# Four graph-attention layers on one core: engines that issue in text order, a third buffer for the rows, and 33-column sums in the third layer

## The chip, the cores and the metric

The kernel runs on one NeuronCore of a Trainium2 chip. The metric is the time of one execution on the device, in microseconds (us). A core has a matrix engine (TensorE, in the profile PE, with its weight loads as PEld), a vector engine (VectorE, DVE), an activation engine (ScalarE, ACT), a general engine (GpSimd, POOL) and a queue that only starts transfers (SyncE, SP). Each takes its own list of instructions in the order in which the compiler has put them, and they wait for each other by semaphores.

## The reference

The input x has 8 batches of 2048 rows with 128 features; adj is a 2048x2048 symmetric 0/1 matrix, shared by all batches. Four layers follow one another, each of the form x = x + layer(relu(layernorm(x))).

- Layers 0 and 1 are graph attention: Wh = h W, a score leaky_relu(f1[i] + f2[j]) for each pair of rows, a softmax over the j that are neighbours of i, and the weighted sum of Wh. Layer 0 ends with elu.
- Layer 2 has no weights: 4 heads of 32 features, score = leaky_relu(h_i . h_j), softmax over neighbours, weighted sum of h itself.
- Layer 3 is graph attention again, with the rows scaled by node weights before it, a layernorm after the projection, that normed value added to the sum, and elu.

```
scores = einsum('bihk,bjhk->bhij', x, x); scores = leaky_relu(scores, 0.2)
probs = softmax(where(adj == 0, -inf, scores)); out = einsum('bhij,bjhk->bihk', probs, x)
```

## The kernel before

**Units.** A unit is one layer of one batch. Even and odd batches form two streams, and the units alternate between them, so that while one unit computes its attention, the next one, of the other batch, is prepared. Numbered in the order of execution: unit 0 is batch 0 layer 0, 1 is batch 0 layer 1, 2 is batch 1 layer 0, 3 is batch 0 layer 2, 4 is batch 1 layer 1, 5 is batch 0 layer 3, 6 is batch 1 layer 2, 7 is batch 2 layer 0, 8 is batch 1 layer 3, 9 is batch 2 layer 1, 10 is batch 3 layer 0, 11 is batch 2 layer 2, and so on with a period of eight; unit 31 is batch 7 layer 3. Units 0 and 1, and 30 and 31, are of the same batch, so that 1 and 31 are prepared with nothing beside them.

**Steps.** A unit has steps, each with a front and a back. For layers 0, 1 and 3 (`Gat`, 16 steps) front(s) makes a tile z of masked attention weights with two VectorE instructions of 128x1024 (L455), and back(s) is 16 matmuls of z against the 129-column y (L468; the last column gives the softmax's denominator). For layer 2 (`Heads`, 4 groups of 512 rows, 16 steps each) front(s) is eight score matmuls (L539, a value split into two parts, hi_lo and lo_hi), two exponentials on ACT (L542) and one mask product on VectorE (L544); back(s) is the sums (L557): for each head a 32-column block of hv and a 32-column block of ones, each in its own 32-column tile of the array. z has three buffers. The text writes front(s+2) ahead of back(s).

**PSUM.** The eight banks are shared out by hand: score pairs start at banks 6, 4 and 2 in turn (`score_banks`), Heads sums in banks 0 and 1, Gat sums of the first eight row blocks in 5, 6, 7 and of the second eight in 2, 1, 0. Preparation uses the single pair 3,4 while a Gat unit runs, and the score pairs in turn while a Heads unit runs.

**Preparation.** `begin` of the next unit is a list of pieces, called one by one after the steps: with P pieces, ceil(P(s+1)/(steps-4)) of them have been called after step s. It has 20 pieces for layers 0 and 1, 17 for layer 2 and 39 for layer 3: the statistics of x, four row blocks at a time (`stats`, L193 and L194), `end` (variance on VectorE, a power on POOL at L201, a product at L203), `rows` (ACT, L245), for layer 3 `scaled` (L252), `turned` (eight transposes L263, copied by ACT), and then `project` (L287), `spread` (L338), and for layer 3 a second round of statistics, `normed` and `weighted`. For layer 2 `kept` copies the rows to hv and `stacked` issues sixteen copies on SP's queue from the two parts of the transposed rows to hi_lo and lo_hi (L277, L278). In a Gat unit that is followed by a Heads unit, front(0) of the latter stands in the text ahead of the last back, and front(1) behind it.

**Ends.** When a half of a Gat unit is done, `out_first` (L396) divides and evacuates it, and `out_elu` or, for layer 3, `out_norm` and then the output's transfer follow some steps later by `later` and `pass_time`. When a group of a Heads unit is done, ACT copies the two banks of sums (L563), and `out` takes the reciprocal of 128x512 denominators (L567), multiplies (L568), transposes (L571) and adds to x (L573).

**Order.** Nothing of this text order binds the engines: a planner, working from estimated costs, priorities and free buffers, chooses the order in which each engine issues, and puts in the semaphores. It follows the text in the middle of a Heads unit and departs from it elsewhere: VectorE's statistics are moved ahead of mask products, PE's transposes and projections behind sums, and the four transposes of L571 some 35 PE instructions back. The eight batches' rows x have two buffers, so that the load of a third batch waits for the output of the first.

Of the kernel before, what the change touches and what calls it, by code (L numbers as in the profile page):

```python
# [8 lines left out]
F32 = mybir.dt.float32  # L9
# [5 lines left out]
OP = mybir.AluOpType  # L15
# [4 lines left out]
HD = 32  # L20
SLOPE = 0.2
# [13 lines left out]
def adj_preln_d4(ctx: ExitStack, tc: tile.TileContext, x, adj, w0, a0, w1, a1, w3, a3,  # L35
# [80 lines left out]
    beta2_sb = const.tile([P, C], F32, name="beta2_sb")  # L116
    nc.vector.tensor_scalar(beta2_sb, beta_sb, 2.0, None, op0=OP.mult)
# [20 lines left out]
    def run(ctx, general):  # L138
# [25 lines left out]
        def load_x(b):  # L164
            X[b] = big.tile([P, NB, C], F32, tag="x", name="x")
            nc.sync.dma_start(out=X[b], in_=x[b].rearrange("(n p) c -> p n c", p=P))
# [21 lines left out]
        hv = held.tile([P, NB, C], F32, name="hv")  # L188
# [17 lines left out]
        class Unit:  # L206
# [5 lines left out]
            def begin(self, banks):  # L212
# [42 lines left out]
                def kept(half):  # L255
                    nc.vector.tensor_copy(hv[:, half * HB:(half + 1) * HB, :], self.hw[half])
# [164 lines left out]
            def out_norm(self, half, xs, a, later):  # L421
                nc.vector.tensor_add(a, a, self.wh[:, half * HB:(half + 1) * HB, :])
                nc.vector.tensor_mul(a, a, gamma_sb[:, None, :].to_broadcast([P, HB, C]))
                nc.vector.tensor_add(a, a, beta2_sb[:, None, :].to_broadcast([P, HB, C]))
# [100 lines left out]
        class Heads(Unit):  # L525
# [22 lines left out]
            def back(self, s, later):  # L548


                g, jb = divmod(s, NB)
                z = self.z.pop(s)
                for bank in range(2):
                    for h in range(HEADS):
                        cols = slice(h * HD, (h + 1) * HD)
                        lhsT = ones[:, cols] if bank else hv[:, jb, cols]
                        nc.tensor.matmul(ps[cols, bank, :], lhsT=lhsT, rhs=z[:, h, :],  # L557
                                         start=(jb == 0), stop=(jb == NB - 1),
                                         tile_position=(0, h * HD))
                if jb == NB - 1:  # L560
                    o_t = big.tile([P, 2, 512], F32, tag="o_t", name="o_t")
                    for bank in range(2):
                        nc.scalar.copy(o_t[:, bank, :], ps[:, bank, :])  # L563
                    later(2.6, lambda: self.out(g, o_t))

            def out(self, g, o_t):
                nc.vector.reciprocal(o_t[:, 1, :], o_t[:, 1, :])  # L567
                nc.vector.tensor_mul(o_t[:, 0, :], o_t[:, 0, :], o_t[:, 1, :])  # L568
                pv = ps[:, score_banks(), :].rearrange("p (k e) -> p k e", k=4)
                for k in range(4):  # L570
                    nc.tensor.transpose(pv[:, k, :], o_t[:, 0, k * P:(k + 1) * P], ident)  # L571
                xs = X[self.b][:, g * 4:g * 4 + 4, :]
# [94 lines left out]
```

## Time and profile before

The median of two runs is 3630.32 us (3630.07 to 3630.56). The profiled execution took 3630.07; its span from the first to the last instruction is 3628.3, and the mean clock granted to TensorE is 0.954.

| | us |
|---|---|
| PE / PEld busy | 3326.6 / 2225.2 |
| DVE / ACT / POOL busy | 2760.0 / 1675.7 / 134.7 |
| L468, Gat sums, PE | 1424.1 |
| L557, Heads sums, PE: hv, ones | 580.3, 572.4 |
| L544 mask, L542 exponentials | 1167.3, 1083.3 |
| L567 reciprocal, 32 of 3346 ns | 107.1 |
| the chain that ended last: PE / DVE / ACT | 65% / 17% / 9% |

The units in the steady part, from the first matmul of one unit's back to that of the next: 3 (Heads) from 347.7 to 559.5, 211.8 long; 4 to 631.1, 71.6; 5 to 706.5, 75.4; 6 (Heads) to 923.7, 217.2; 7 to 995.1, 71.4; 8 to 1060.0, 64.9; 9 to 1132.2, 72.2; 10 to 1215.8, 83.6. Unit 28 takes 72.5 and unit 1 65.4; unit 30 computes from 3314.0 to 3516.2.

In a group's line the mean of one instruction is in ns, and "idle before" is the time its engine stood ahead of it, with the releaser that ended it. In a timeline, the first two numbers are start and length in us, "x8" is so many instructions taken together, and the bracket is the idle time ahead. A float32 matmul appears as two passes, so that L557 has 4096 entries for 2048 matmuls. PE busy is not PE at its peak, as overlapping matmuls count once.

### The profile page before, as it was taken

To read this page: it belongs to the slowest core of one execution; us is meant where nothing else is said; L and a number is where in the kernel's file an instruction comes from. 1 tells how busy PE (TensorE), PEld (TensorE's weight loads), DVE (VectorE), ACT (ScalarE), POOL (GpSimd) and SP (SyncE) were. 2 spreads that over 40 slices of the span, in tenths; PEclk is the share of its full clock that TensorE was granted. 3 is DMA by queue.
4 is the path that set the end of the run, shared out by engine and by line. 5 is a ranking of instruction groups with operands and counts; after the bars stand their busy time and mean duration, and the time that the engine had idled before them with its cause. 6 is when DMAs were issued, how large, how long until landed. Compare 5 with 4: busy or idle time off the path is not lost.

```text
span 3628.3 us, 61084 instructions
## 1 busy us (share of the span) xinstructions
PE 3326.6 (92%) x26637; PEld 2225.2 (61%) x26637; DVE 2760.0 (76%) x3490; ACT 1675.7 (46%) x2521; POOL 134.7 (4%) x46
## 2 busy tenths in 40 slices
PE   4798999999999899989999899999999989999987
PEld 3796338733899334943499733783379943495337
DVE  3666778777887677867797677877788768787876
ACT  4214663376422564256442366426642256524652
POOL 0000000000000000000000000000000000010000
PEclk7888999999999899989999899999999989999998
DMA  6002000300000200030000200020000020002000
GB/s 212 1 1 47 1 1 1 71 1 1 1 24 5 43 1 1 1 70 1 1 1 24 47 1 1 1 71 1 1 1 7 19 47 1 1 1 59 1 1 13
DMA packets 35541, 71.46 MB, mean 20 GB/s; under 512 B 8000, under 2 KB 25024, under 8 KB 29120
## 3 DMA queue, kind: packets, MB, share of 16 engines
q1 hardware_dynamic: 29312, 67.12, 7.2%
q8 instruction: 210, 3.44, 0.4%
q10 hardware_dynamic: 5952, 0.35, 0.1%
q14 instruction: 67, 0.55, 0.0%
HBM read 25.51 MB, written 8.39 MB: 9 GB/s over the span
## 4 chain that ended last, share of the span: by engine, by line
PE 65%; DVE 17%; ACT 9%; issue 3%; POOL 3%; DMA 2%; POOLq 0%; ACTq 0%; DVEq 0%; SPq 0%
PE ps L468 28%; PE ps L557 20%; PE ps L539 12%; ACT z L542 5%; DVE z L544 5%; DVE z L455 4%; DVE o_t L567 3%; PE ps L287 2%; POOL rstdx L201 2%; PE ps L263 2%; ACT wh L321 1%; PE ps L338 1%; ACT hw L245 1%; DVE stx L193 1%; POOL rstdh L201 1%
## 5 line engine op out<-in xcount | busy, mean ns | idle before, releaser
L544 DVE TENSOR_TENSOR z<-z,edge_t 128x2048 f32<-128x2048 f32 x512 | 1167.3, 2288 | 396.2 <-ACT z L542 396.1
L468 PE MATMUL ps<-y,z 128*128 128x129 f32 x12288 | 1424.1, 277 | 4.0 <-DVE z L455 4.0
L468 PEld LDWEIGHTS ps<-y,z 128*128 128x128 f32 x12288 | 1405.5, 193 | 14.7 <-DVE z L455 5.9
L542 ACT ACTIVATE z<-ps,shift 128x1024 f32<-128x1024 f32 x1024 | 1083.3, 1113 | 492.7 <-PE ps L539 471.5
L455 DVE SCALAR_TENSOR_TENSOR z<-r,cr,edge_t 128x1024 f32<-128x1024 f32 x768 | 951.7, 1275 | 86.1 <-PE ps L468 73.6
L557 PE MATMUL ps<-z,hv 128*32 128x512 f32 x4096 | 580.3, 615 | 25.2 <-DVE z L544 23.0
L539 PE MATMUL ps<-hi_lo 64*128 64x512 f32 x2048 | 497.3, 461 | 111.9 <-ACT z L542 103.4
L557 PE MATMUL ps<-z,ones 128*32 128x512 f32 x4096 | 572.4, 599 | 0.0
L539 PEld LDWEIGHTS ps<-hi_lo 64*128 64x128 f32 x2048 | 206.3, 188 | 565.9 <-ACT z L542 433.9
L245 ACT ACTIVATE hw<-x,nmrx,rstdx 128x128 f32<-128x128 f32 x512 | 203.7, 482 | 547.3 <-DVE nmrx L203 547.3
L539 PE MATMUL ps<-lo_hi,hi_lo 64*128 64x512 f32 x2048 | 432.1, 402 | 0.0
L557 PEld LDWEIGHTS ps<-z,ones 128*32 128x32 f32 x4096 | 136.8, 111 | 311.7 <-issue 310.9
L539 PEld LDWEIGHTS ps<-lo_hi,hi_lo 64*128 64x128 f32 x2048 | 214.5, 191 | 22.1
L557 PEld LDWEIGHTS ps<-z,hv 128*32 128x32 f32 x4096 | 85.0, 108 | 226.8 <-issue 155.3
L201 POOL TENSOR_TENSOR rstdx<-varx,neg_half 128x16 f32<-128x16 f32 x32 | 104.2, 3258 | 3206.5 <-DVE varx L199 3206.5
L263 PE MATMUL ps<-ident,hw 128*128 128x128 f32 x512 | 96.1, 305 | 54.4 <-ACT hw L245 26.7
L193 DVE BATCH_NORM_STATS2 stx<-x 128x6 f32<-128x128 f32 x512 | 127.6, 268 | 12.6 <-DMA x<-in_x_dram 11.6
L412 ACT ACTIVATE oe<-ps,rs 128x128 f32<-128x128 f32 x128 | 52.4, 409 | 177.5 <-DVE rs L405 177.5
L287 PEld LDWEIGHTS ps<-rhs,h_t 128*128 128x128 f32 x768 | 102.3, 204 | 49.1 <-issue 14.3
L287 PE MATMUL ps<-rhs,h_t 128*128 128x130 f32 x768 | 120.5, 300 | 10.2 <-DVE y L299 6.7
L415 ACT ACTIVATE oa<-ps,rs 128x128 f32<-128x128 f32 x128 | 35.3, 380 | 180.1 <-DVE rs L405 180.1
L263 PEld LDWEIGHTS ps<-ident,hw 128*128 128x128 f32 x512 | 66.3, 150 | 77.7 <-ACT hw L245 30.6
(89 smaller groups left out, 1267.7 us busy)
## 6 DMA issues: line engine op xcount, KB each, us to landing
raw<-in_adj_dram SPq DMA_DIRECT2D x16, 1024.0 KB, 7.3
hi_lo<-h_hi SPq DMA_DIRECT2D x32, 256.0 KB, 5.1
hi_lo<-h_lo SPq DMA_DIRECT2D x32, 256.0 KB, 5.1
lo_hi<-h_lo SPq DMA_DIRECT2D x32, 256.0 KB, 5.1
lo_hi<-h_hi SPq DMA_DIRECT2D x32, 256.0 KB, 5.2
out_dram<-x SPq DMA_DIRECT2D x16, 512.0 KB, 3.3
w_sb<-in_L_gnn_W_dram ACTq DMA_DIRECT2D x3, 64.0 KB, 2.3
x<-in_x_dram SPq DMA_DIRECT2D x8, 0.5 KB, 6.4
```

The costliest lines, as they stand in the source:

```text
L193: nc.vector.bn_stats(out=st[:, n, :], in_=block(n))
L201: nc.gpsimd.tensor_tensor(out=rstd, in0=var, in1=neg_half, op=OP.pow)
L245: nc.scalar.activation(h, self.xb[:, n, :], AF.Relu, scale=self.rstd[:, n:n + 1], bias=self.nmr[:, n:n + 1])
L263: nc.tensor.transpose(pk[:, k, :], self.hw[half][:, k, :], ident)
L287: nc.tensor.matmul(pv[:, k, :C + 2], lhsT=self.h_t[:, n * P:(n + 1) * P], rhs=rhs, start=True, stop=True)
L455: nc.vector.scalar_tensor_tensor(z[:, j, :], self.r[:, sl], self.cr[:, 0, jb:jb + 1], edge_t[:, jb, sl], op0=OP.max, op1=OP.mult)
L468: nc.tensor.matmul(ps[:, SUMS[half][i // 3], k * CE:(k + 1) * CE], lhsT=z[:, j, i * P:(i + 1) * P], rhs=self.y[:, jb, :], start=(jb == 0 a ...
L539: nc.tensor.matmul(ps[:, lo + h, :], lhsT=hi_lo[rows, pair, js], rhs=rhs[rows, pair, ts], start=rhs is hi_lo, stop=rhs is lo_hi)
L542: nc.scalar.activation(z[:, pair * 2:pair * 2 + 2, :], ps[:, lo:lo + 2, :], AF.Exp, bias=shift)
L544: nc.vector.tensor_mul(z, z, edge_t[:, jb, None, ts].to_broadcast([P, HEADS, 512]))
L557: nc.tensor.matmul(ps[cols, bank, :], lhsT=lhsT, rhs=z[:, h, :], start=(jb == 0), stop=(jb == NB - 1), tile_position=(0, h * HD))
L567: nc.vector.reciprocal(o_t[:, 1, :], o_t[:, 1, :])
```

## The change

Four things change together.

- Inside the branch that runs, PE, ACT and DVE issue in the order of the text (`manual_schedule`). SP and POOL keep the planner's order.
- x has three buffers. To make room, twice beta is computed in place.
- hv gets 33 columns a head, the last one 1.0 (a memset on POOL at the start); `kept` copies into the first 32 of each.
- The sums of a head are one matmul with 33 columns, two heads to a bank, at partitions 0 and 64; four matmuls instead of eight. `out` is called for each pair of heads: four transposes, a reciprocal of the 128x8 denominators, a product into a new tile, and the sum into x; each call takes a turn of the score banks.

```diff
-            X[b] = big.tile([P, NB, C], F32, tag="x", name="x")
+            X[b] = big.tile([P, NB, C], F32, tag="x", name="x", bufs=3)
...
-        hv = held.tile([P, NB, C], F32, name="hv")
+        hv = held.tile([P, NB, HEADS, HE], F32, name="hv")
+        nc.gpsimd.memset(hv[:, :, :, HD:HE], 1.0)
...
-                for bank in range(2):
-                    for h in range(HEADS):
-                        cols = slice(h * HD, (h + 1) * HD)
-                        lhsT = ones[:, cols] if bank else hv[:, jb, cols]
-                        nc.tensor.matmul(ps[cols, bank, :], lhsT=lhsT, rhs=z[:, h, :],
-                                         start=(jb == 0), stop=(jb == NB - 1),
-                                         tile_position=(0, h * HD))
-                if jb == NB - 1:
-                    o_t = big.tile([P, 2, 512], F32, tag="o_t", name="o_t")
-                    for bank in range(2):
-                        nc.scalar.copy(o_t[:, bank, :], ps[:, bank, :])
-                    later(2.6, lambda: self.out(g, o_t))
-
-            def out(self, g, o_t):
-                nc.vector.reciprocal(o_t[:, 1, :], o_t[:, 1, :])
-                nc.vector.tensor_mul(o_t[:, 0, :], o_t[:, 0, :], o_t[:, 1, :])
-                pv = ps[:, score_banks(), :].rearrange("p (k e) -> p k e", k=4)
+                for pair in range(2):
+                    for h in range(2):
+                        nc.tensor.matmul(ps[h * 64:h * 64 + HE, pair, :],
+                                         lhsT=hv[:, jb, pair * 2 + h, :], rhs=z[:, pair * 2 + h, :],
+                                         start=(jb == 0), stop=(jb == NB - 1))
+                    if jb == NB - 1:
+                        o_t = big.tile([P, 512], F32, tag="o_t", name="o_t")
+                        nc.scalar.copy(o_t, ps[:, pair, :])
+                        later(2.6, lambda o_t=o_t, pair=pair: self.out(g, pair, o_t))
+
+            def out(self, g, pair, o_t):
+                lo = score_banks()
+                pv = ps[:, lo, :].rearrange("p (k e) -> p k e", k=4)
                 for k in range(4):
-                    nc.tensor.transpose(pv[:, k, :], o_t[:, 0, k * P:(k + 1) * P], ident)
-                xs = X[self.b][:, g * 4:g * 4 + 4, :]
-                nc.vector.tensor_add(xs, xs, pv)
+                    nc.tensor.transpose(pv[:, k, :], o_t[:, k * P:(k + 1) * P], ident)
+                pv = pv.rearrange("p k (h e) -> p k h e", h=2)
+                r = stat.tile([P, 4, 2, 1], F32, tag="r2", name="r2")
+                nc.vector.reciprocal(r, pv[:, :, :, HD:HE])
+                o = big.tile([P, 4, 2, HD], F32, tag="o", name="o", bufs=1)
+                nc.vector.tensor_mul(o, pv[:, :, :, :HD], r.to_broadcast([P, 4, 2, HD]))
+                xs = X[self.b][:, g * 4:g * 4 + 4, pair * 64:(pair + 1) * 64]
+                nc.vector.tensor_add(xs, xs, o.rearrange("p k h d -> p k (h d)"))
...
+            inner.enter_context(tc.manual_schedule(engines={
+                mybir.EngineType.PE, mybir.EngineType.Activation, mybir.EngineType.DVE}))
             run(inner, False)
```

## The prediction

> **What bounds the kernel now.** I read the page first (shares, slices), then the stretches unit by unit (units are numbered in the text above), then timelines of single steps. The page:
>
> ```profile
> PE 3326.6 (92%) x26637; PEld 2225.2 (61%) x26637; DVE 2760.0 (76%) x3490; ACT 1675.7 (46%) x2521; POOL 134.7 (4%) x46
> ...
> PE   4798999999999899989999899999999989999987
> PEld 3796338733899334943499733783379943495337
> DVE  3666778777887677867797677877788768787876
> ```
>
> PE is busy 92% on average, but the share is not one limit throughout. Units 4, 8, 9 and 30 (columns: length, then busy us of PE, PEld, DVE, ACT):
>
> ```profile
> 559.50:631.10 71.60, 66.51 (x585) 65.07 (x582) 64.43 (x142) 19.61 (x44) 7.65 (x2) 1.00 0.01 1
> ...
> 995.10:1060.00 64.90, 64.78 (x578) 64.40 (x577) 52.65 (x67) 19.86 (x59) 3.78 (x1) 1.00 0.03 9
> 1060.00:1132.20 72.20, 68.22 (x578) 67.48 (x577) 57.22 (x107) 15.15 (x40) 3.78 (x1) 0.95 0.08 23
> ...
> 3314.00:3516.20 202.20, 197.30 (x1520) 69.92 (x1520) 160.54 (x96) 132.84 (x130) 0.00 (x0) 0.99 0.00 1
> ```
>
> Unit 8 is PE and nothing else. Unit 4, a Gat unit that prepares a layer-3 unit, is VectorE: 64.43 busy and two waits of 2.79 for POOL's rstd make 70.0 of 71.6. A Heads step is PE's:
>
> ```profile
> 423.44 2.29 DVE L544 TENSOR_TENSOR z<-z,edge_t 128x2048 f32<-128x2048 f32 x1 [0.69 <-ACT z L542]
> 423.50 0.50 PE L539 MATMUL ps<-hi_lo 64*128 64x512 f32 x2
> ...
> 424.30 2.12 ACT L542 ACTIVATE z<-ps,shift 128x1024 f32<-128x1024 f32 x2 [0.88 <-PE ps L539]
> ...
> 424.63 1.06 PE L557 MATMUL ps<-z,hv 128*32 128x512 f32 x8
> 425.51 1.04 PE L557 MATMUL ps<-z,ones 128*32 128x512 f32 x8
> 426.48 0.50 PE L539 MATMUL ps<-hi_lo 64*128 64x512 f32 x2
> ```
>
> 2.98 us a step, of which the sums take 424.63 to 426.48, 1.85; the mask (2.29) and the exponentials (2.12) fit beneath. A Gat step is 3.57 (16 matmuls in two passes, "x128" in 14.3 for four steps) over 2.46 of VectorE. So 24 x 57.2 + 8 x 190.7 = 2898 of the 3628.3; the rest is preparation and stalls. The two places where PE stands:
>
> ```profile
> 1172.40 1.04 PE L263 MATMUL ps<-ident,hw 128*128 128x128 f32 x8
> ...
> 1176.51 1.22 DVE L268 TENSOR_TENSOR h_lo<-ps,h_hi 128x1024 fp32r<-128x1024 f32 x1
> ...
> 1193.94 1.28 SPq L278 DMA_DIRECT2D lo_hi<-h_hi  x1
> ...
> 1207.60 0.79 PE L539 MATMUL ps<-hi_lo 64*128 64x512 f32 x1 [12.94 <-ACT z L542]
> ```
>
> Gat to Heads (unit 10): the copies into hi_lo and lo_hi go out at about 1.25 apiece, and PE waits 12.94 for exponentials queued behind other ACT work. The end of a Heads group:
>
> ```profile
> 3363.60 3.34 DVE L567 RECIPROCAL o_t<-o_t 128x512 f32<-128x512 f32 x1
> ...
> 3369.15 1.04 PE L557 MATMUL ps<-z,hv 128*32 128x512 f32 x2 [1.01 <-DVE z L544]
> 3370.12 0.66 PE L571 MATMUL ps<-ident,o_t 128*128 128x128 f32 x4
> ```
>
> The reciprocal holds the mask. Unit 30 is 202.2 against 190.7: 11.5 for three group ends inside it, 3.8 each.
>
> **What the Trainium skill says.** "TensorEngine Tiling (Array Packing)", Available Configurations: 128x32 gives four tiles, 128x64 two, working independently. The trace agrees for four: eight passes begin 0.88 apart per set of four heads, two slots of 0.43. No row shows two of 64. "TensorE: Matmul & The Clock Gate", the table at its head: ACT and VectorE queues are strict FIFO, PE pulls only weight loads ahead; so an instruction that waits holds all behind it. The 12.94 agrees. Same page, Part 1: some 3.4 us of idling halves the clock. Agrees: after that stall hv's eight took 1.94 for 1.06.
>
> **The sums (L557).** Removed: eight matmuls in four-wide tiles, four slots of 0.43. Added: four with 33 columns, two-wide: again 8 passes / 2 = four slots. Unchanged at 1.85, if two 64-column tiles run side by side. Bound: from 0 to +1.7 a step (one after another, 8 x 0.43 = 3.44), 512 steps. I take 0.
>
> **Group ends.** Removed: L567 (3.34), L568 (0.68), L573 (0.69), four transposes. Added, for each pair: four transposes (0.53 to 0.66), a reciprocal of 128x8 (0.17, as L405), a product and a sum of 128x256 (0.4 each, from L573's 0.69 for twice the size), and a second turn of the score banks. In text order they stand right after the last sums: PE waits for the ACT copy behind the second exponential (0.55), transposes twice (1.15), and the second score pair waits 0.6 for the bank that VectorE still reads. 2.35 for 3.8: -1.45, x32 = -46.
>
> **The order.** All stretches below are the text laid out by hand with these durations: z pair 2.46; statistics of four blocks 1.5 (a dependent pair of L193 and L194 is 0.38, where the planner's interleaving shows 0.29); "end" 3.8 to 4.2 (POOL 2.90 to 3.79 and both semaphores), during which VectorE stands with everything behind it; scaled 1.1; weighted 0.69; norm_end 5.0. Pieces fall at ceil(count(s+1)/12) a step.
> Unit 4 (39 pieces): on VectorE, out 1.9, z(2) 4.4, three statistics 8.9, z(3) 11.4, statistics and end 16.7, z(4) 19.2. PE has done back(3) at 15 and waits 4.2 for z(4); then 1.2 for turned, 1.1 and three times 1.0 in project, since bank pair 3,4 is single: back(7) ends at 44.5. VectorE then does recips, products, norm_stats and norm_end up to 60.8, z(11) at 63.3: PE waits 2.6 and 5.4, two spreads 3.2, four more steps: 84.4 for 71.6. Before, 12 of the 16 statistics were done in the Heads unit's VectorE slack. Same for unit 7 (71.4). +12.9 each; ends +6 to +16.
> Unit 8 (20 pieces), on VectorE: z(2), a statistic and unit 7's out_elu 6.4; z(3) 8.9; two statistics 11.9; z(4) and a statistic 15.9; z(5) and end 22.5; z(6) 25.0. PE, with back(5) from 18.4, has done it at 22.0 and waits 3.0 for z(6) (0.5 before that). So 57.2, 8.8 of PE pieces (two turned of 1.1, four projects of 1.15, two spreads of 1.0), 3.5, and 2.6 where two pieces on bank pair 3,4 stand in one step = 72.1 for 64.9, +7.2. Unit 9 is the same with out_norm (3.7) and out_elu (2.4) of layer 3 in its first three steps: waits of 7.3 for 3.5, 75.9 for 72.2, +3.7.
> Unit 10: 41.3 to the second turned, +3.7 behind layer 1's L409s and end. Then front(0) stands in the text before back(15). The copies land 20.9 after L268 ends (1177.7 to 1198.6), L268 ends 2.3 after turned: 23.2, and PE is there after four steps, 14.3. So it waits 8.4, with back(15) behind it; back(15) ends at about 29.8 (3.57 and 2.5 of slow clock), the copies out of banks 2,1,0 and the exponential of front(1) hold back(0) for 5.1 more: 34.9 for 42.4. 79.9 for 83.6, -3.7. Unit 5: the out DMA ahead of the copies on SP's queue makes the same wait 13: 82.6 for 75.4, +7.2.
> Units 3, 6: 190.7, four ends 9.4, PE pieces 9.7, end 1.2, and 2 in unit 6 for out_norm: 211.0 and 213.0 for 211.8 and 217.2: -0.8, -4.2.
> Sum of units 3 to 10: +35.2 (2 x 12.9 + 7.2 + 3.7 - 3.7 + 7.2 - 0.8 - 4.2). Three such rounds: +105.6. Units 27 to 30: -0.8 + 11.9 + 7.2 + 0 (ends -5.8, the unhidden start of unit 31 +6). Unit 0: x's statistics now follow all sixteen edge casts, +9. Units 1, 2: +4.5, -3.7. Together +134.
>
> **The third x buffer.** SP waited 17.2 in six loads for the out DMA. Text order would put VectorE behind such a load; with three buffers the load stands at the unit's start, hidden by the unit before. Nothing taken; up to 9 (6.1 landing, 3.2) in each of three units if it is issued late.
> **Else.** The hv copy with a gap every 32 (16 x 0.7), the memset and doubling beta in place: nothing, at most 7 on VectorE in Heads slack.
>
> 3628.3 + 134 = 3762, and 1.8 around the span as before (3630.07 for 3628.3): **3764**. The profiled run is 0.25 below the median, nothing at this size.
>
> **Rivals.**
> Faster: the wait at Gat to Heads goes. If the copies have landed when PE comes to front(0), it leaves Gat at once: units of type 10 lose 17.3, of type 5 11, four each, -113, with the ends -46: 3471 if VectorE also keeps up, 3496 with half the cost of units 8 and 9 (16) and unit 0's start (9). It decides at 14.3 us from turned to the last landing; 23.2 measured speaks against. 0.09.
> Balanced: VectorE keeps its two z ahead, as its total falls by 107 + 22 + 22 (L567, L568, L573) against some 60 added; then units 4 and 7 cost +4 (7 x 9 less) and 8 and 9 half (16 less): 3685, within 3590 to 3703. Unit 4's 70.0 of 71.6 speaks against: what the order takes from the Heads units has no room there. 0.17.
> Serial tiles: the 64-column tiles take turns: +1.6 to 1.7 x 512 less some VectorE waits it hides: 4600. 0.08.
> That the order is not what the text says is excluded for steady Heads steps, where both orders are the same.
>
> **How the numbers follow.** Forecast 0.66, 3703 to 3860, with units 4 and 7 and tile switches at their ends. Range 3590 to 3860 leaves out faster and serial. A measurement tells about 2% (73 us) from no change: slower 0.66 + 0.08, same 0.17, faster 0.09.
>
> **What would show it.** L557 still 1.85 a step, statistics evenly in Gat units, PE waiting for z L455 there some 10 us a unit; L539 waiting for the copies' DMA before the last Gat step; no 3.3 us reciprocal. Wrong if unit 4 stays near 72, or a Heads step isn't 2.98.

## The result, and the profile after

The changed kernel takes 3789.27 us (median of 2 runs, 3787.88 to 3790.66) for 3630.32 before: a ratio of 1.0438, 95% interval 1.0393 to 1.0483. It is slower by 159 us. The forecast was 3764 and slower; the sum was 25 us short, with one stall not foreseen, others mis-sized and two terms that were set at nothing. The profiled execution took 3787.88, its span is 3786.1, and the mean clock granted to TensorE 0.944 (0.954 before).

The page after: engine totals, TensorE's slices, and the two groups of matmuls with the most idle time ahead of them (the last figures of a group line are that idle time, with its releasers). The same two groups before stand below.

```profile
PE 3325.6 (88%) x22669; PEld 2246.7 (59%) x22669; DVE 2743.8 (72%) x3586; ACT 1681.6 (44%) x2521; POOL 117.0 (3%) x47
...
PE   4798998799899899979988899888989989988986
...
L471 PE MATMUL ps<-y,z 128*128 128x129 f32 x12288 | 1465.4, 282 | 115.3 <-DVE z L458 114.9
...
L542 PE MATMUL ps<-hi_lo 64*128 64x512 f32 x2048 | 473.6, 452 | 127.4 <-DMA hi_lo<-h_lo 50.5
```

Before:

```profile
L468 PE MATMUL ps<-y,z 128*128 128x129 f32 x12288 | 1424.1, 277 | 4.0 <-DVE z L455 4.0
...
L539 PE MATMUL ps<-hi_lo 64*128 64x512 f32 x2048 | 497.3, 461 | 111.9 <-ACT z L542 103.4
```

PE is busy for the same time as before (3326.6), VectorE for 16 us less, ACT for 6 more: over the whole span, the 158 us are time in which PE stands. Gat's sums now wait 115 us, nearly all of it for VectorE's z, where they waited 4. The first passes of the scores wait 127 us for 112, so there it is mainly the reasons that changed: exponentials before, and now the copies with 50 as the largest of three. The second passes (lo_hi) wait 25.5 us for the copies, where they waited for nothing, and the projections (L290, L287 before) wait 43.7 for 10.2.

A wait also costs what comes after it. Gat's sums are the same matmuls as before and are busy for 1465.4 us instead of 1424.1. Cut into short stretches, the profile has a granted clock of 1.00 in steady steps (401 to 404) and of 0.5 to 0.6 behind the long waits (0.51 from 588.7 to 594.0 in unit 4). That PE's total did not rise is owed to the changed kernel's other matmuls: without the text's order it keeps PE busy for 3306.9 only, at a clock of 0.961 (the run of the sums and the buffer below).

Unit by unit, from one back's first matmul to the next (us):

| units | before | forecast | after |
|---|---|---|---|
| start of unit 0, and unit 0 | 102.0 + 96.7 | 9 more | 107.5 + 100.2 |
| 3 (Heads) | 211.8 | 211.0 | 210.9 |
| 4 (Gat, prepares layer 3) | 71.6 | 84.4 | 84.9 |
| 5 | 75.4 | 82.6 | 81.1 |
| 6 (Heads, behind layer 3) | 217.2 | 213.0 | 219.5 |
| 7 | 71.4 | 84.3 | 85.2 |
| 8 | 64.9 | 72.1 | 72.9 |
| 9 | 72.2 | 75.9 | 74.2 |
| 10 | 83.6 | 79.9 | 81.6 |
| 30 with the preparation of 31 | 240.0 | 240.2 | 249.5 |

The steady Heads step is what it was. In the timeline (start, length, instruction, idle time ahead) the masks of two steps stand 2.97 apart (2.98 before). The eight passes of the 33-column sums take 1.91 to their end and 1.84 to the start of the next scores (401.46 to 403.30), where the eight and eight of before took 1.85 to the next scores.

```profile
401.46 1.91 PE L556 MATMUL ps<-z,hv 128*33 128x512 f32 x8
...
403.30 0.50 PE L542 MATMUL ps<-hi_lo 64*128 64x512 f32 x2
...
428.48 2.29 DVE L547 TENSOR_TENSOR z<-z,edge_t 128x2048 f32<-128x2048 f32 x1 [0.67 <-ACT z L545]
...
431.45 2.29 DVE L547 TENSOR_TENSOR z<-z,edge_t 128x2048 f32<-128x2048 f32 x1 [0.68 <-ACT z L545]
```

The first end of a group in unit 3:

```profile
404.43 1.91 PE L556 MATMUL ps<-z,hv 128*33 128x512 f32 x8
406.08 1.07 ACT L561 COPY o_t<-ps 128x512 f32<-128x512 f32 x2
...
406.72 1.14 PE L568 MATMUL ps<-ident,o_t 128*128 128x128 f32 x8 [0.38 <-ACT o_t L561]
...
408.43 0.17 DVE L200 TENSOR_SCALAR varx<-mvx 128x16 f32<-128x16 f32 x1
...
408.77 2.90 POOL L202 TENSOR_TENSOR rstdx<-varx,neg_half 128x16 f32<-128x16 f32 x1 [110.92 <-DVE varx L200]
411.70 0.18 DVE L204 SCALAR_TENSOR_TENSOR nmrx<-mvx,rstdx 128x16 f32<-128x16 f32 x1 [3.10 <-POOL rstdx L202]
...
412.03 0.42 DVE L573 TENSOR_TENSOR o<-ps,r 128x256 f32<-128x256 f32 x1
...
412.51 0.50 PE L542 MATMUL ps<-hi_lo 64*128 64x512 f32 x2 [3.98 <-DVE o L573]
...
413.26 3.46 PE L556 MATMUL ps<-z,hv 128*33 128x512 f32 x8
```

The 3.34 us reciprocal is gone, and at the next two ends PE stands 0.6 at the scores where here it stands 3.98. What makes this one long is `end`: the variance, POOL's power and the product stand in the text ahead of `out`, VectorE waits for POOL, and the product L573 that frees the bank of the next scores waits behind it. The sums that follow then take 3.46 for 1.91, as the granted clock is 0.54 from 413.2 to 416.7.

The two unit types that lost most are 4 and 7. In unit 4, VectorE works off twelve blocks of statistics in a row (from 575.15), and then `end`:

```profile
579.91 2.45 DVE L458 SCALAR_TENSOR_TENSOR z<-r,cr,edge_t 128x1024 f32<-128x1024 f32 x2
581.21 3.84 PE L471 MATMUL ps<-y,z 128*128 128x129 f32 x32 [1.20 <-DVE z L458]
...
583.99 0.18 DVE L200 TENSOR_SCALAR varx<-mvx 128x16 f32<-128x16 f32 x1
584.34 2.90 POOL L202 TENSOR_TENSOR rstdx<-varx,neg_half 128x16 f32<-128x16 f32 x1 [172.67 <-DVE varx L200]
587.27 0.17 DVE L204 SCALAR_TENSOR_TENSOR nmrx<-mvx,rstdx 128x16 f32<-128x16 f32 x1 [3.10 <-POOL rstdx L202]
587.37 2.47 DVE L458 SCALAR_TENSOR_TENSOR z<-r,cr,edge_t 128x1024 f32<-128x1024 f32 x2
...
588.70 1.66 PE L471 MATMUL ps<-y,z 128*128 128x129 f32 x6 [3.64 <-DVE z L458]
...
631.34 2.87 PE L471 MATMUL ps<-y,z 128*128 128x129 f32 x12 [4.47 <-DVE z L458]
```

PE stands for 1.20 and 3.64 here, for 1.16 and 4.47 around `norm_end` (the last line), and four times for 0.9 to 1.1 at transposes and projections: 14.4 in all. The unit as a whole (length, busy us of PE, PEld, DVE, ACT, POOL, then clock, share of the DMA engines, GB/s):

```profile
569.10:654.00 84.90, 70.47 (x578) 68.84 (x577) 65.94 (x152) 19.24 (x43) 5.80 (x2) 0.94 0.00 1
```

Before, unit 4 had PE busy for 66.51 of 71.6 at a clock of 1.00. So of the 13.3 us that it lost, 9.3 are more waiting and 4.0 are matmuls that took longer behind the waits.

Unit 6 holds what the forecast did not have:

```profile
742.40 1.22 DVE L427 TENSOR_TENSOR oa<-oa,beta_sb 128x1024 f32<-128x1024 f32 x1
743.72 1.06 ACT L429 ACTIVATE oe<-oa 128x1024 f32<-128x1024 f32 x1 [6.26 <-DVE oa L427]
744.81 1.06 ACT L430 ACTIVATE oa<-oa 128x1024 f32<-128x1024 f32 x1
745.77 4.11 ACT L545 ACTIVATE z<-ps,shift 128x1024 f32<-128x1024 f32 x4
746.92 0.79 PE L542 MATMUL ps<-hi_lo 64*128 64x512 f32 x2 [6.22 <-ACT z L545]
```

`out_norm` of unit 5 issues an exponential and a relu on ACT behind three VectorE instructions, and those stand behind two masks. ACT waits for them, the score exponentials L545 wait behind ACT's two, and PE stands for 6.22 us. It is so in units 6, 14, 22 and 30.

In unit 8 the longest wait is a projection (L290) that needs the single bank pair 3,4:

```profile
1082.75 1.06 ACT L430 ACTIVATE oa<-oa 128x1024 f32<-128x1024 f32 x1
...
1084.03 0.69 DVE L302 TENSOR_TENSOR y<-ps,y 128x512 f32<-128x512 f32 x1
...
1084.77 1.51 PE L290 MATMUL ps<-rhs,h_t 128*128 128x130 f32 x8 [3.46 <-DVE y L302]
```

At the turn from Gat to Heads (unit 2), the scores of front(0) stand ahead of the last sums:

```profile
339.10 0.79 PE L542 MATMUL ps<-hi_lo 64*128 64x512 f32 x1 [2.00 <-DMA hi_lo<-h_lo]
...
344.13 0.76 PE L542 MATMUL ps<-hi_lo 64*128 64x512 f32 x1 [4.25 <-DMA hi_lo<-h_lo]
...
346.55 0.76 PE L542 MATMUL ps<-lo_hi,hi_lo 64*128 64x512 f32 x1 [1.53 <-DMA lo_hi<-h_hi]
...
347.24 5.91 PE L471 MATMUL ps<-y,z 128*128 128x129 f32 x32
```

With the 1.22 before them these waits make 9.0, and the sums that had been ready then run in 5.91 for 3.57, at a granted clock of 0.64.

### The profile page after: what moved, and what is told of

The parts are those of the page before. It is cut to its first block, busy times and chain, and to the rows that moved or that the text cites. A ratio compares the mean times of both kernels' runs of the same rounds, so it can differ in the third digit from the quotient of the medians.

```text
span 3786.1 us, 53159 instructions
## 1 busy us (share of the span) xinstructions
PE 3325.6 (88%) x22669; PEld 2246.7 (59%) x22669; DVE 2743.8 (72%) x3586; ACT 1681.6 (44%) x2521; POOL 117.0 (3%) x47
## 4 chain that ended last, share of the span: by engine, by line
PE 62%; DVE 18%; ACT 5%; issue 2%; POOL 2%; SPq 2%; DMA 1%; POOLq 0%; DVEq 0%; ACTq 0%
PE ps L556 22%; PE ps L471 22%; PE ps L542 14%; DVE z L458 8%; ACT z L545 2%; PE ps L290 2%; DVE z L547 2%; POOL rstdx L202 2%; DMA lo_hi<-h_hi 1%; DVE stx L194 1%; DVE mvx L195 1%; PE ps L341 1%; PE ps L266 1%; SPq L280 1%; SPq L281 1%
## 5 line engine op out<-in xcount | busy, mean ns | idle before, releaser
L471 PE MATMUL ps<-y,z 128*128 128x129 f32 x12288 | 1465.4, 282 | 115.3 <-DVE z L458 114.9
L471 PEld LDWEIGHTS ps<-y,z 128*128 128x128 f32 x12288 | 1445.0, 199 | 131.5 <-DVE z L458 128.0
L545 ACT ACTIVATE z<-ps,shift 128x1024 f32<-128x1024 f32 x1024 | 1087.7, 1114 | 610.5 <-PE ps L542 605.7
L556 PE MATMUL ps<-z,hv 128*33 128x512 f32 x4096 | 995.0, 608 | 8.2 <-DVE z L547 8.2
L542 PE MATMUL ps<-hi_lo 64*128 64x512 f32 x2048 | 473.6, 452 | 127.4 <-DMA hi_lo<-h_lo 50.5
L556 PEld LDWEIGHTS ps<-z,hv 128*33 128x33 f32 x4096 | 197.8, 111 | 531.7 <-issue 495.3
L246 ACT ACTIVATE hw<-x,nmrx,rstdx 128x128 f32<-128x128 f32 x512 | 206.0, 488 | 559.9 <-DVE nmrx L204 559.9
L542 PE MATMUL ps<-lo_hi,hi_lo 64*128 64x512 f32 x2048 | 419.9, 397 | 25.5 <-DMA lo_hi<-h_hi 25.5
L542 PEld LDWEIGHTS ps<-lo_hi,hi_lo 64*128 64x128 f32 x2048 | 199.4, 188 | 53.6 <-issue 24.8
L290 PE MATMUL ps<-rhs,h_t 128*128 128x130 f32 x768 | 118.1, 302 | 43.7 <-DVE y L302 21.6
L290 PEld LDWEIGHTS ps<-rhs,h_t 128*128 128x128 f32 x768 | 102.3, 207 | 75.3 <-DVE y L302 24.7
L266 PE MATMUL ps<-ident,hw 128*128 128x128 f32 x512 | 77.6, 292 | 41.4 <-ACT hw L246 24.5
L195 DVE BATCH_NORM_AGGREGATE mvx<-stx 128x2 f32<-128x6 f32 x512 | 93.2, 182 | 17.8
L302 DVE TENSOR_TENSOR y<-ps,y 128x512 f32<-128x512 f32 x64 | 44.1, 688 | 84.1 <-ACT cr L397 83.9
```

The source lines that it names most:

```text
L195: nc.vector.bn_aggr(out=mv[:, n, :], in_=st[:, n, :])
L246: nc.scalar.activation(h, self.xb[:, n, :], AF.Relu, scale=self.rstd[:, n:n + 1], bias=self.nmr[:, n:n + 1])
L266: nc.tensor.transpose(pk[:, k, :], self.hw[half][:, k, :], ident)
L290: nc.tensor.matmul(pv[:, k, :C + 2], lhsT=self.h_t[:, n * P:(n + 1) * P], rhs=rhs, start=True, stop=True)
L471: nc.tensor.matmul(ps[:, SUMS[half][i // 3], k * CE:(k + 1) * CE], lhsT=z[:, j, i * P:(i + 1) * P], rhs=self.y[:, jb, :], start=(jb == 0 a ...
L542: nc.tensor.matmul(ps[:, lo + h, :], lhsT=hi_lo[rows, pair, js], rhs=rhs[rows, pair, ts], start=rhs is hi_lo, stop=rhs is lo_hi)
```

## Experiments: which part of the change costs

The theory: the text's order is the cause, VectorE's above all; the sums are neutral in the steady step and cheaper at group ends; the third buffer is worth nothing. The rivals: the two-wide sums are the cause; or PE's and ACT's order is.

**The order with the old sums.** The kernel before, with the third buffer (and, to make room, o_t with one buffer and twice beta in place) and the text's order.

```diff
-            X[b] = big.tile([P, NB, C], F32, tag="x", name="x")
+            X[b] = big.tile([P, NB, C], F32, tag="x", name="x", bufs=3)
...
-                    o_t = big.tile([P, 2, 512], F32, tag="o_t", name="o_t")
+                    o_t = big.tile([P, 2, 512], F32, tag="o_t", name="o_t", bufs=1)
...
+            inner.enter_context(tc.manual_schedule(engines={
+                mybir.EngineType.PE, mybir.EngineType.Activation, mybir.EngineType.DVE}))
```

> The kernel before with its own sums (eight matmuls in 32-column tiles, the 128x512 reciprocal), a third buffer for x (one buffer fewer for o_t makes the room) and the text's order on PE, ACT and DVE. Theory (the order is the cause): at least as slow as the changed kernel, because the whole loss of 159 us is the order's, and the group ends, which the new sums made cheaper, stay: the reciprocal of 3.34 us then stands between the last sums and the transposes with nothing moved into its place, 32 ends of some 5 us where the changed kernel has some 2.3 to 4: 3810 to 3900 us. Rival (the two-wide sums are what costs): near 3630, within 40.

Measured: 3975.76 us, ratio 1.0941 (1.0923 to 1.096), past the upper end of what the theory gave. Heads units take 236 to 246, where the changed kernel's take 209 to 220. The first end of a group in its unit 3, in its timeline:

```profile
412.69 3.35 DVE L566 RECIPROCAL o_t<-o_t 128x512 f32<-128x512 f32 x1
416.07 0.69 DVE L567 TENSOR_TENSOR o_t<-o_t 128x512 f32<-128x512 f32 x1
...
416.91 1.09 PE L570 MATMUL ps<-ident,o_t 128*128 128x128 f32 x4 [9.66 <-DVE o_t L567]
```

The planner had moved these transposes some 35 PE instructions back, so that PE had other work during the reciprocal; in the text they follow the last sums and PE stands 9.66 here, 6.3 to 6.9 at the other three ends.

**The sums and the buffer without the order.** The changed kernel without the two lines of `manual_schedule`.

```diff
-            inner.enter_context(tc.manual_schedule(engines={
-                mybir.EngineType.PE, mybir.EngineType.Activation, mybir.EngineType.DVE}))
```

> The changed kernel with its 33-column sums and its third buffer, but all engines in the planner's order. Theory (order): the loss is gone, 3580 to 3640 us; a Heads step stays 2.98 and the group ends fall from 3.8 to some 2, up to 46 us less than before if the planner moves work into the ends. Rival (the sums are the cause): 3750 to 3790.

Measured: 3550.23 us, ratio 0.9775 (0.9758 to 0.9791). The sums are not the cause; with the planner, sums and buffer make the kernel 80 us faster than before, which is below the range that the theory gave. Its Heads units take 206.0 to 207.1, with PE idle for 0.7 in each.

**The buffer alone**, in the planner's order, with the old sums, o_t with one buffer and twice beta in place.

```diff
-            X[b] = big.tile([P, NB, C], F32, tag="x", name="x")
+            X[b] = big.tile([P, NB, C], F32, tag="x", name="x", bufs=3)
...
-                    o_t = big.tile([P, 2, 512], F32, tag="o_t", name="o_t")
+                    o_t = big.tile([P, 2, 512], F32, tag="o_t", name="o_t", bufs=1)
```

> The kernel before, in the planner's order and with its own sums, with a third buffer for x (and one buffer fewer for o_t). Theory (of the 80 us by which the 33-column sums with the buffer beat the kernel before, the Heads units hold 65, so the sums have most of it): 3605 to 3632, with Heads units still at 211 to 218 us; the loads of x no longer wait. Rival (the buffer is most of it): 3555 to 3585.

Measured: 3614.40 us, ratio 0.9952 (0.9936 to 0.9969). So of the 80 us the buffer has 16 and the sums 64, where the group ends had been put at 46. The 16 are small but not nothing: units 6, 14 and 22, where the third batch's rows are loaded, fall from 217.2, 218.0 and 218.3 to 212 each. The buffer also shifts time between units: unit 8 rises from 64.9 to 69.7 and unit 9 falls from 72.2 to 64.6, with nothing in text order.

The books of the change are therefore: buffer -16, sums -64, order +239; together +159. Taken with the order ahead of the sums, they are buffer -16, order +361 and sums -186. What the sums are worth depends on the order: with the planner they save 64 us, in the text's order 186, as there the old ends stand in the open.

**The order on part of the engines.** The changed kernel with the text's order on PE and ACT alone, and on VectorE alone.

```diff
-                mybir.EngineType.PE, mybir.EngineType.Activation, mybir.EngineType.DVE}))
+                mybir.EngineType.PE, mybir.EngineType.Activation}))
```

> The changed kernel with the text's order on PE and ACT alone; VectorE is in the planner's order. Theory (VectorE's order, with the statistics and the variance-power-product chain standing ahead of z, is most of it: units 4, 7, 8, 9 and the group ends that wait behind the power): some 100 of the 159 us come back, 3640 to 3700, and unit 4 (84.9 us) falls below 77. Rival (PE's and ACT's order is the cause: front(0) of Heads ahead of the last Gat step, transposes behind waits): 3740 to 3790, with unit 4 still above 82.

```diff
-                mybir.EngineType.PE, mybir.EngineType.Activation, mybir.EngineType.DVE}))
+                mybir.EngineType.DVE}))
```

> The changed kernel with the text's order on VectorE alone; PE and ACT are in the planner's order. Theory (VectorE's order is most of it): 3710 to 3780 us, unit 4 stays at 80 to 85 and units 8 and 9 at 70 to 75, since PE has nothing to put in place of sums whose z is late. Rival (PE's and ACT's order is the cause): 3630 to 3680, unit 4 below 77.

Measured: 3625.57 (ratio 0.998, 0.9971 to 0.9988) with PE and ACT in text order; 3709.81 (1.0209, 1.0192 to 1.0226) with VectorE. Both lie below the ranges expected, the second by less than 1 us. Against the 3550 of the planner the first costs 75 us and the second 160, and both together 239: in the total they add up. VectorE's order is two thirds of the loss. But not everywhere, and unit by unit the two do not simply add (us):

| unit | planner | PE, ACT in text | VectorE in text | all in text |
|---|---|---|---|---|
| 4 | 71.4 | 75.6 | 80.4 | 84.9 |
| 5 | 76.9 | 81.6 | 78.0 | 81.1 |
| 6 | 206.6 | 210.3 | 217.1 | 219.5 |
| 7 | 67.3 | 75.7 | 82.2 | 85.2 |
| 8 | 70.8 | 72.9 | 66.9 | 72.9 |
| 9 | 64.6 | 67.0 | 70.4 | 74.2 |

Units 4, 6, 7 and 9 are mostly VectorE's. Units 5 and 8 are not: with VectorE alone in text order unit 8 takes 66.9, against 70 to 75 expected, and with PE and ACT the full 72.9. Against the planner's 70.8 with the same sums and buffer, that is 2 us. PE's order and ACT's were not taken apart.

## Experiments: the single stalls

Each of the next four edits is made to the changed kernel, text order on all three engines; they move lines of the text and take no wait away.

**The product after POOL's power as a piece of its own**, called behind the next front (and the same for layer 3's norm).

```diff
                 add(end)
                 add(lambda: None)
+                add(end_b)
...
-                    add(norm_end)
-                    add(lambda: None)
+                    add(norm_end_a)
+                    add(lambda: None)
+                    add(lambda: None)
+                    add(norm_end)
```

Here `end` and `norm_end_a` stop at the power, `end_b` is L204, and `norm_end` goes on from there. The lists of pieces grow by one, for layer 3 by three, so that later pieces shift as well; what that does was not separated.

> The changed kernel; the product after POOL's power (nmr) is a piece of its own that the text calls after the next front, instead of right behind the power, for the statistics of x and of layer 3's projection. Theory (VectorE stands behind POOL with z and the group ends behind it): units 4 and 7 lose 3 to 6 us each of 85, each Heads unit 1.5 to 3 (the 3.98 us gap at one group end goes), units 8 and 9 up to 3: 3789 - 60 = 3730, within 3705 to 3760. Rival (VectorE in units 4 and 7 is simply full, and the power's wait only moves the same work): the units stay within 1 us and the time is 3775 to 3795.

Measured: 3722.62 us, ratio 1.0256 (1.0239 to 1.0273): 67 less, as the theory's number had it, from other places than it said. Heads units fall by 5 to 8 us each (unit 3 to 205.4, unit 6 to 211.7), units 2 and 10 by 4, and in unit 3 no wait at the scores of a group end is over 0.62. Units 4 and 7, where 3 to 6 each were expected, stay, as the rival had it for them: 84.4 and 86.2. The wait for POOL does shrink there, from 3.10 to 1.60, and the next takes its place:

```profile
578.23 3.78 POOL L202 TENSOR_TENSOR rstdx<-varx,neg_half 128x16 f32<-128x16 f32 x1 [169.38 <-DVE varx L200]
...
582.04 0.18 DVE L207 SCALAR_TENSOR_TENSOR nmrx<-mvx,rstdx 128x16 f32<-128x16 f32 x1 [1.60 <-POOL rstdx L202]
...
584.19 2.47 DVE L471 SCALAR_TENSOR_TENSOR z<-r,cr,edge_t 128x1024 f32<-128x1024 f32 x2
586.58 2.13 DVE L259 TENSOR_SCALAR hw<-hw,nw_sb,nb_sb 128x128 f32<-128x128 f32 x8
586.98 1.25 PE L272 MATMUL ps<-ident,hw 128*128 128x128 f32 x4 [2.32 <-DVE hw L259]
...
588.02 6.20 PE L484 MATMUL ps<-y,z 128*128 128x129 f32 x32
```

PE now stands 2.32 at the transposes (L272, `turned`), whose rows come late down the same chain: statistics, power, product, rows, scaling. The sums stand behind them until 588.02, though their z L471 was done at 586.7 (584.19 and 2.47), and then run in 6.20 for 3.57. So POOL's wait ended PE's wait in unit 4, but taking half of it away did not shorten the unit.

**Twelve of layer 3's sixteen statistics in the Heads unit before**, behind the `out` of its first three groups. `early_part` computes those of four row blocks, into a tile that the layer-3 unit takes over.

```diff
-                for q in range(4):
+                for q in range(3 if layer == 3 else 0, 4):
                     add(stats, q)
...
                 nc.vector.tensor_add(xs, xs, o.rearrange("p k h d -> p k (h d)"))
+                if pair == 1 and g < 3:
+                    if g == 0:
+                        early[self.b] = stat.tile([P, NB, 2], F32, tag="mve", name="mve", bufs=1)
+                    early_part(early[self.b], X[self.b], g)
```

> The changed kernel; 12 of the 16 statistics of x for a layer-3 unit stand in the text in the Heads unit before, behind each group's out, instead of in unit 4 or 7. Theory (what the text's order took from the Heads units has no room on VectorE in units 4 and 7): units 4, 7 and their like (seven) lose 4.5 to 9 us each, the Heads units gain up to 1.5 at each of three group ends: net -20 to -55, 3735 to 3770. Rival (it is not the load but the position of the waits): units 4 and 7 within 2 us, the time 3780 to 3825.

Measured: 3767.14 us, ratio 1.0382 (1.0364 to 1.0399), 22 less: within the theory's span at its weak end, but unit by unit below it. Unit 4 goes from 84.9 to 81.3, unit 7 from 85.2 to 83.8, unit 30 with its preparation from 249.5 to 243.8. Less work on VectorE in units 4 and 7 buys 3.6 and 1.4 us, of the 13 to 14 lost and the 4.5 to 9 expected.

**The first front of Heads behind the last back of Gat.**

```diff
-                elif overlaps and s == u.steps - 1:
-
-                    turn[0] = 2
-                    nxt.front(0)
                 u.back(s, later)
+                if overlaps and u.layer != 2 and nxt.layer == 2 and s == u.steps - 1:
+                    turn[0] = 2
+                    nxt.front(0)
```

> The changed kernel; where a Heads unit follows a Gat unit, front(0) of the Heads unit stands in the text behind the last back of the Gat unit instead of ahead of it. Theory (PE waits 8.4 for the copies with a ready sum behind it, which then runs at half clock): 3 to 6 us less at each of eight such places, 3741 to 3765. Rival (the landing of the copies sets the start of the Heads unit in either order): within 8 of 3789.

Measured: 3735.41 us, ratio 1.0293 (1.0276 to 1.031), 54 less, more than the 24 to 48 expected. Units of type 10 fall from 81.6 to 73.9, of type 5 from 81.1 to 75.9. PE's one long wait for the copies, 5.88, now has the finished sums ahead of it, and unit 3's first sums follow at 353.37:

```profile
347.30 0.76 PE L542 MATMUL ps<-hi_lo 64*128 64x512 f32 x1 [5.88 <-DMA hi_lo<-h_lo]
...
353.37 1.91 PE L556 MATMUL ps<-z,hv 128*33 128x512 f32 x8 [0.19 <-DVE z L547]
```

**out_norm's exponential and relu later.** The 5.0 of `later` are counted off at 2.7 a Heads step and 4.0 a Gat step, so that the two stand two steps later in the text, and with them `out_elu` and the output's transfer.

```diff
-                nc.scalar.activation(e, a, AF.Exp)
-                nc.scalar.activation(a, a, AF.Relu)
+                def acts():
+                    nc.scalar.activation(e, a, AF.Exp)
+                    nc.scalar.activation(a, a, AF.Relu)
+                    later(6.0, last)
...
-                later(6.0, last)
+                later(5.0, acts)
```

> The changed kernel; the exponential and the relu of layer 3's out_norm stand in the text one step later than its three VectorE instructions. Theory (ACT waits for those three, and the exponentials of the scores behind it hold PE 6.2 us in unit 6 and its like): units 6, 14 and 22 fall from 219.5 to 213 to 215, 3770 to 3777 in all. Rival (the masks behind the three VectorE instructions are what PE waits for): the gap stays and the time is within 5 of 3789.

Measured: 3736.83 us, ratio 1.0297 (1.028 to 1.0314), 52 less for 12 to 19 expected. The gap goes: in unit 6 ACT's L431 now waits 0.80, and PE's longest stop at this place is 1.76 behind a mask.

```profile
742.82 1.06 ACT L431 ACTIVATE oe<-oa 128x1024 f32<-128x1024 f32 x1 [0.80 <-DVE oa L427]
...
745.04 1.91 PE L559 MATMUL ps<-z,hv 128*33 128x512 f32 x8 [1.76 <-DVE z L550]
```

Unit 6 falls to 212.1, as do 14 and 22, and unit 30 loses 7: some 29 of the 52. The rest is in units of type 5 (2.6 each) and 9 (3.7 each) and was not traced to an instruction; the later `out_elu` may have part in it. Unit 8, where layer 3's first half ends, gains nothing (72.8).

**All four together.**

> The changed kernel, text order on all three engines, with four edits to the text together: nmr in a piece of its own, early statistics for layer 3, the first front of Heads behind the last Gat back, out_norm's ACT work a step later. Theory (they are separate stalls and add up): 67 + 22 + 54 + 52 = 195 off 3789, 3594, within 3575 to 3625; unit 4 stays above 78, as none of them evens out what falls on VectorE in a step. Rival (they are one stall seen in four places, the next wait takes over): 3645 to 3690.

Measured: 3577.38 us, ratio 0.9844 (0.9827 to 0.986): 212 less than the changed kernel, where the four alone add up to 195. So they are separate stalls: in the total, none of the gains was lost to a wait behind it. The text's order with these edits, the sums and the buffer is 1.6% below the kernel before, and still 27 us above the planner's order with the sums and the buffer alone. The sums' wait for z is 26.1 for 115.3. Unit 4 stays at 80.7 and unit 7 at 79.4.

**The four edits, with VectorE in the planner's order.**

```diff
-                mybir.EngineType.PE, mybir.EngineType.Activation, mybir.EngineType.DVE}))
+                mybir.EngineType.PE, mybir.EngineType.Activation}))
```

> The run with the four edits to the text, with the text's order on PE and ACT alone; VectorE is in the planner's order. Theory (what is left of the text's cost is VectorE's in units 4, 7 and 9 and at the start, and the edits hold what PE and ACT wait for at the turn to Heads): units 4, 7, 9 at 75.6, 75.7 and 67 for 80.7, 79.4 and 69.5, unit 0 with its start 8 less, units 2, 5 and 10 stay at 70 to 71: 3577 - 48 = 3529, within 3505 to 3550, less than the 3550 of the planner on all engines. Rival (the planner's VectorE brings back what the edits took away): 3560 to 3600.

Measured: 3544.80 us, ratio 0.9765 (0.9749 to 0.9781). It is within its range, but not for its reasons: units 4 and 7 come to 78.7 and 77.5, not 75.6, and the 5 us by which it beats the planner on all engines (3550.23) are inside the intervals. The two are the fastest that were run, some 2.3% below the kernel before.

**Every second copy on POOL's queue.** The turn to Heads waits for sixteen copies that go out on SP's queue 1.25 us apart. Is it the issuing that paces them? The kernel is that of the sums and the buffer in the planner's order.

```diff
-                            nc.sync.dma_start(out=tf[at + HD:at + 64, pair, :],
-                                              in_=second[rows_, :])
+                            nc.gpsimd.dma_start(out=tf[at + HD:at + 64, pair, :],
+                                                in_=second[rows_, :])
```

> The run with the 33-column sums, the third buffer and the planner's order, with every second of the sixteen copies into hi_lo and lo_hi issued on POOL's queue instead of SP's. Theory (the issue of sixteen copies at 1.25 us each is what lands them 20.9 us after their source is ready): landing in 11 to 14 us, units 2, 10 and their like fall from 83.6 by 5 to 10 us, units 5 and 13 from 77 by 3 to 8, 3485 to 3520. Rival (the exponentials queued behind other ACT work hold the start of Heads whenever the copies land, or POOL issues more slowly): 3540 to 3560.

Measured: 3562.78 us, ratio 0.9813 (0.9797 to 0.983): 13 more than on one queue. The theory fell. The stretches from the second copy's issue to the landing of the last (the last issue, 693.18, and the 5.2 that a copy takes; in the other run up to PE's next pass on lo_hi, 689.70, shortly after the last landing at 689.3 by the trace's semaphores) in unit 5 (columns: stretch, length, busy us of PE, PEld, DVE, ACT, POOL, clock, share of the DMA engines' time, GB/s), first on one queue. A 512 KB transfer of the output lies in both:

```profile
676.10:698.40 22.30, 14.93 (x97) 11.94 (x97) 12.10 (x13) 6.41 (x12) 0.00 (x0) 0.86 0.98 216
```

and on two:

```profile
667.10:689.70 22.60, 11.88 (x83) 10.72 (x81) 6.84 (x6) 0.10 (x1) 3.38 (x7) 0.77 0.82 193
```

One queue already keeps the sixteen DMA engines busy for 98% of the stretch, at 216 GB/s with the output's transfer. The copies by themselves, in unit 10 before, keep them busy for 90%, at 189 GB/s:

```profile
1177.70:1198.60 20.90, 16.11 (x131) 14.71 (x130) 9.61 (x24) 4.24 (x16) 0.00 (x0) 0.96 0.90 189
```

On two queues POOL issues its eight in 6.1 us (664.41 to 670.52), and SP's then take 1.6 to 2.7 apiece:

```profile
670.03 0.49 POOL L281 DMA_DIRECT2D lo_hi<-h_hi  x1
...
673.99 2.74 SPq L280 DMA_DIRECT2D hi_lo<-h_hi  x1
```

So the 1.25 us is the pace of the transfers (256 KB at 216 GB/s are 1.21 us), shown by the issuing queue. This is what the Trainium skill's "DMA: Bandwidth & Descriptors" says under Issuing engines are not separate DMA queues: that transfers started by different engines run on the same sixteen DMA engines, and only the issuing time is saved. This run agrees: 22.6 us for 22.3. With two queues at work a single copy took longer to land (medians 7.0 to 10.9 us for 5.1), and front(0) in unit 5 waits 9.96 for one of its first: 84.9 for 76.9, while unit 2 gained 6. Issuing half of the copies from ACT instead of POOL was not tried.

## Why the prediction was right, point by point

- **The sums, step kept at 1.85: right** (1.84 to the next scores, step 2.97). Eight passes of 0.43 one after another would take 3.44, so the two 64-column tiles run side by side; the serial rival of 4600 is out.
- **Group ends, 2.35 each for 3.8: right.** In unit 30 as it computes, 202.8 less 190.7 less the 6.2 of `out_norm` leaves 5.9 for three ends, 2.0 each. Missed was that one end in each Heads unit meets `end`: 3.98 where the others have 0.6. The forecast had counted `end` in a Heads unit at 1.2; it is 3.4. Unit 3 still came out at 210.9 for 211.0, since the plain ends were cheaper. Moving the product away took 5 to 8 us from each Heads unit that prepares another, more than the wait itself; some 1.5 us of that are the sums that ran in 3.46 for 1.91 behind it.
- **Unit 4, 84.4: right in size** (84.9), and in the view: 4.84 of PE waits for z in the first part where 4.2 was worked out, 5.63 in the norm for 8.0. The reason given, POOL's wait with z behind it, holds as what ends the wait. That this wait sets the unit's length is not borne out, for with it halved the unit keeps its length and PE stands at the transposes instead. So the number is in part luck: the forecast had the waits for z 1.7 us too long and left out the 4.0 us of slower matmuls. What does shorten the unit is VectorE's order given back (75.6) and earlier statistics (81.3). What holds it at 80.7 with all four edits was not found.
- **Unit 8, 72.1: right number (72.9) by luck, wrong step.** It was laid out as VectorE falling behind with z. The trace has one such wait, 1.72; the largest, 3.46, is a projection that waits for the bank pair 3,4, which the product L302 still reads, and the next sums stand behind it on PE. L302 was late as its exponentials stood on ACT behind `out_norm`'s two; with those two moved it is late behind `out_norm` and z on VectorE, and PE waits 3.30. With VectorE alone in text order this wait is gone and the unit takes 66.9, so PE's or ACT's place in the order is part of it; as moving ACT's two gained nothing, PE's place for the projection is the likelier, but that was not tried alone. The forecast also put all of the rise to the text's order. The third buffer by itself takes unit 8 to 69.7 and unit 9 to 64.6 in the planner's order, so that the text's order costs some 2 to 3 us in unit 8 and 10 in unit 9 (74.2), not 7.2 and 3.7.
- **The turn to Heads: right.** A wait of 8.4 was forecast and 9.0 measured; units 10 and 5 took 81.6 and 81.1 for 79.9 and 82.6. The order of front(0) and the last back costs 54 us over the eight turns.
- **Unit 6, 213.0: wrong, 219.5.** This is the step that failed: "2 in unit 6 for out_norm" costed its VectorE instructions and not the two on ACT, which stand ahead of the score exponentials. 6.22 us in four units; with the two moved, unit 6 takes 212.1.
- **The end, +6 for the start of unit 31: too small.** From the last sums of unit 30 to the first of 31 are 46.7 us for 37.9 before, +8.8. With 6.2 of `out_norm` and 5.6 less for the three ends this is the +9.5 of unit 30, for which nothing was forecast.
- **The start, +9: right** (5.5 and 3.5), and for its reason: the first statistics of x start at 71.1, where the casts end, and stood at 25.1 before.
- **The rivals.** Faster, 3471, hung on the copies having landed; PE waits 9.0 for them. Balanced, 3685, hung on VectorE keeping its lead in unit 4; it takes 84.9, not 75.6. The kernel that does keep it there, with VectorE in the planner's order, takes 3626.
- **The third buffer, nothing: wrong by 16 us** in the planner's order. In the text's order the prediction had it only delay VectorE. By the text it is more than that: in unit 6 the first statistics of batch 2 are called after step 3, ahead of the `out_elu` of the second half of batch 0. With two buffers these statistics wait for a load, that load for the output of batch 0, and that output for the `out_elu` behind the statistics on VectorE. So the text's order should need the third buffer; this is argued from the text and was not tried.

The total came near because it was built from the stretches of one trace, by laying out the text's order with measured durations. It was short by 25. Units 6, 14, 22 and 30 together, those with `out_norm`, came out 27 us over their forecasts; each of the others was within 3.1 of its own, and these misses cancel to -3.

## What to carry to other kernels

When an order is bound to the text, walk the text once for each engine, ACT and PE too, and ask of every instruction that can wait what stands behind it: here edits at four places, of a few lines each, took back 212 us where the order had cost 239. A wait that a profile names is where the delay came to light; before costing its removal, ask what the same late chain holds next. And a change of several parts is to be split on the chip: here two parts gained 80 us and the third lost 239, and the gain of one part tripled with the order that it ran in.

## What the runs showed of the hardware that was not expected

- Sixteen copies of 256 KB between SBUF rows keep the DMA engines 90% busy at 189 GB/s, and 98% at 216 GB/s with a 512 KB output among them; a second issuing queue lands them no earlier (22.6 us for 22.3).
- POOL's 128x16 power takes 2.90 us when VectorE stands still as it starts, even if a mask product follows on VectorE 0.4 us later and runs beside it (405.95 to 408.85 in the run with the product split off). In that run 22 of the 40 powers take 3.72 to 3.78. Each of these starts while VectorE is in a scalar_tensor_tensor (of Gat's z or of `out_elu`), and is longer by what is left of that instruction, less 0.14 us (0.88 for 1.02). So it is not VectorE's work as such that counts but what runs as the power starts; no run has a mask product running there. The mean over the powers of x rose from 2.90 to 3.50 with the split, so part of what the wait gave back was lost there.
- A wait of PE's costs more than its length. Behind the 3.64 us in unit 4 the granted clock is 0.51 from 588.7 to 594.0, and behind the turn to Heads and the group end of unit 3 the sums took 5.91 for 3.57 and 3.46 for 1.91.
- To the next scores, the sums of a step take 1.84 us as eight passes in two 64-column tiles and 1.85 as sixteen in four 32-column tiles: half the instructions, the same time.
